# A transformer block on one core: output projection, second norm and feed-forward placed earlier in a software pipeline

## The chip, the cores and the metric

The kernel runs on one core of one Trainium2 chip. The metric is device time in microseconds; the time of the kernel before is the median of three runs. The profile is of one further execution, recorded by the hardware profiler. Engines are called PE (TensorE), DVE (VectorE), ACT (ScalarE), POOL (GpSimd) and SP (SyncE, which here only issues transfers).

## The reference

The input `x` has 16 sequences of 256 rows and 256 columns, all in fp32. One block with the norm ahead of each part is computed:

```
x = x + attention(layernorm(x))      # 16 heads of 16, wq, wk, wv, wo are 256 x 256
x = x + ffn(layernorm(x))            # silu(h @ gate.T) * (h @ up.T) @ down.T, inner size 1024
```

In attention a row `i` sees the columns up to `i + 16`: scores above that are set to minus infinity before the softmax. The weights `gate`, `up` and `down` are not given; each is interpolated (cubic, Catmull-Rom) from a vector of some 2033 control points.

## The kernel before, in words

One sequence is one batch `b`, and its 256 rows are two chunks of 128 partitions. Work on a batch is cut into stages that are functions in the code, and a software pipeline runs different stages of different batches in one step `s` of the main loop (L578). In step `s`, `pb = s` is projected to queries, keys and values; `nb = s - 1` has its row maxima found; `tb = s - 2` has its scores computed transposed, exponentiated and multiplied with the values; `ob = s - 3` is divided by its row sums, projected with `wo`, added to `x` and normed again; the feed-forward follows. The order within a step is written out by hand (L578 to L620), and a helper (`InOrder`, L78) keeps each engine in the order of the program, so no scheduler changes it. That helper issues every instruction, which is why all rows of the profile name L88.

The stages that matter here:

- `inner(nb, tb, g)` for four groups of heads and `outer(nb, tb, g2)` for two pairs: PE computes scores for both batches into two PSUM tiles (`scores`), ACT takes the exponentials (`e`), POOL masks them, DVE finds the maxima (`mx`, the rows `z<-scores`). The next scores overwrite the same PSUM tiles.
- `values` (L383): PE multiplies exponentials with values into `po`, ACT copies it to `au`. `gather` (L402) moves `au` into `den` and `ac` with 12 transfers; `invert` (L418) takes the reciprocal of the row sums and spreads it over partitions through DRAM (`rd`, `rb`); `divide` (L432) multiplies, on DVE: `ac<-ac,rb`.
- `project_o` (L436): PE `py<-wo,ac`, then DVE adds it to `x`. `stats_f` and `norm_f` (L450, L453) compute moments on DVE, a power on POOL (`rstdf`) and the normed `xnf` on DVE. `turn_f` (L456) transposes on PE (`ptf`) and copies to `x2T` on ACT.
- `gate_up(b, i)` (L461), four parts of a batch: PE `pg` and `pu`, ACT tanh (`th`), DVE two products, the last into `inter`. `down(b, c)` (L483), two parts: PE `pd`, DVE adds it to `x`; after the second the output is sent from SP.
- `project_v` (L257): PE `pv`, two ACT copies into `v`. `turn_max` (L372): PE transposes the maxima (`pm`), ACT copies `mxT`, and SP sends it with four transfers into a row of the queries (`qk`) that the scores of the next step read.
- `fill(s, gap)` (L553): what goes into seven numbered gaps between these stages. In the first steps the table `heads` (L541) says how many parts of the weights' interpolation (`pw`) and how many idle matmuls go there; the idle matmuls (`keep_running`, L548, named `run`) multiply the identity and are not used. In later steps `fill` puts parts of `gate_up` there.

Before the change the feed-forward of a batch runs over two steps. Step `s` holds `turn_f(s - 4)` and `gate_up(s - 5, 3)` near its start, `gate_up(s - 4, 0)`, `(s - 4, 1)` and `(s - 4, 2)` further on, and `down(s - 5, 0)` and `down(s - 5, 1)`; the second `down` ends the step. [...]

Of the kernel before, what the change touches and what calls it, by code (L numbers as in the profile page):

```python
# [11 lines left out]
F32 = mybir.dt.float32  # L12
# [6 lines left out]
P = 128  # L19
B, S, DIM = 16, 256, 256  # L20
# [73 lines left out]
def block_kernel(  # L94
# [13 lines left out]
    pe, dve, act, pool, sp = (  # L108
        InOrder(tc, e) for e in (nc.tensor, nc.vector, nc.scalar, nc.gpsimd, nc.sync)
    )  # L110

    const = ctx.enter_context(tc.tile_pool(name="const", bufs=1))
    sb = ctx.enter_context(tc.tile_pool(name="sb", bufs=2))
    sb1 = ctx.enter_context(tc.tile_pool(name="sb1", bufs=1))
    sb3 = ctx.enter_context(tc.tile_pool(name="sb3", bufs=3))
    sb4 = ctx.enter_context(tc.tile_pool(name="sb4", bufs=4))
    sb6 = ctx.enter_context(tc.tile_pool(name="sb6", bufs=6))
    sbx = ctx.enter_context(tc.tile_pool(name="sbx", bufs=10))
    dr = ctx.enter_context(tc.tile_pool(name="dr", bufs=2, space=bass.MemoryType.DRAM))
    ps_s = ctx.enter_context(tc.tile_pool(name="ps_s", bufs=1, space=PSUM))  # L120
    ps_f = ctx.enter_context(tc.tile_pool(name="ps_f", bufs=2, space=PSUM))
# [3 lines left out]
    xs = {}  # L125
# [59 lines left out]
    xns, xnTs, mxs, aus, aos, recs, x2s, x2Ts = ({} for _ in range(8))  # L185
# [25 lines left out]
    def transposed(src, dst, nm):  # L211

        pt = ps_m.tile([P, 2, S], F32, tag="m", name=f"p{nm}")
        for kc in range(2):
            for c in range(2):
                pe.transpose(
                    pt[:, kc, c * P : (c + 1) * P],
                    src[:, c, kc * P : (kc + 1) * P],
                    ident,
                )  # L220
        act.copy(dst, pt)
# [62 lines left out]
    def scores(qk, maxima, g, first, to, n):  # L284

        half = slice(first % P, first % P + HB)
        for r in range(4):
            q4 = slice(32 * r, 32 * r + HD + (0 if maxima else 1))
            on = 0 if maxima else 1
            pe.matmul(  # L290
                tiles[r // 2][half, r % 2, to : to + n],
                lhsT=qk[q4, on, g, first : first + HB],
                rhs=qk[q4, 1 - on, g, 0:n] if maxima else qk[q4, 0, g, S - n : S],
                start=True,
                stop=True,
            )

    def find_max(b, g, r, c, at, n):
        h = 4 * g + r
        seen = sb.tile([P, S], BF16, tag="seen", name=f"z{b}_{h}_{c}")  # L300
        dve.tensor_tensor_reduce(
            out=seen[:, 0:n],
            in0=tiles[r // 2][:, r % 2, at : at + n],
            in1=masks[c],
            scale=1.0,
            scalar=NEG,
            op0=ALU.add,
            op1=ALU.max,
            accum_out=mxs[b][:, c, h : h + 1],
        )  # L310

    def inner(nb, tb, g):
        has_n, has_t = 0 <= nb < B, 0 <= tb < B
        qn, qt = qks[nb % NQK], qks[tb % NQK]
        if has_n:
            if g == 0:
                mxs[nb] = sb.tile([P, 2, H], F32, tag="mx", name=f"mx{nb}")
            scores(qn, True, g, P, S, P + HB + LOOK)
        if has_t:
            scores(qt, False, g, HB, HB - LOOK, S - HB + LOOK)  # L320
        if has_n:
            scores(qn, True, g, P + HB, S, S)
        if has_t:
            scores(qt, False, g, 0, 0, S)
        if has_t:
            for pr in range(2):
                e = sb6.tile([P, 2, S], F32, tag="e0", name=f"e0{tb}_{g}_{pr}")
                act.activation(e, tiles[pr][:, :, 0:S], AF.Exp)

                pool.affine_select(  # L330
                    out=e[:, :, 0:M0], in_=e[:, :, 0:M0],
                    compare_op=ALU.is_ge, fill=0.0, base=LOOK,
                    pattern=[[0, 2], [1, M0]], channel_multiplier=-1,
                )
                es[tb, 0, g, pr] = e
        if has_n:
            for r in range(4):
                find_max(nb, g, r, 1, S, S)
# [115 lines left out]
        x2s[b] = normed(b, "f")  # L454

    def turn_f(b):  # L456
        x2Ts[b] = sb3.tile([P, 2, S], F32, tag="x2T", name=f"x2T{b}")
        transposed(x2s.pop(b), x2Ts[b], f"tf{b}")


# [22 lines left out]
    def down(b, c):  # L483
        inter = inters[b]
        pd = ps_f.tile([P, DIM], F32, tag="f", name=f"pd{b}_{c}")
        for ic in range(8):
            pe.matmul(
                pd,
                lhsT=inter[:, ic, c * P : (c + 1) * P],
                rhs=downT[:, ic, :],  # L490
                start=(ic == 0),
                stop=(ic == 7),
            )
        dve.tensor_tensor(xs[b][:, c, :], xs[b][:, c, :], pd, ALU.add)
        if c == 1:
            sp.dma_start(out[b].rearrange("(c p) d -> p c d", p=P), xs.pop(b))

# [9 lines left out]
    def spline(w, part):  # L507
        at = slice(NPART * part, NPART * part + NPART)
        places = tab_in[:, NPART + P * part : NPART + P * part + P]

        pw = [
            pool_.tile([P, NPART], F32, tag=tag, name=f"pw{w}_{part}_{kc}_{piece}")
            for kc, (pool_, tag) in enumerate(((ps_f, "f"), (ps_m, "m")))
            for piece in range(2)
        ]
        for q in range(4):
            rows = slice(32 * q, 32 * q + 32)
            pe.matmul(
                pw[q], lhsT=places[rows], rhs=cp_in[rows, w, :], start=True, stop=True
            )  # L520
        for kc in range(2):
            first, other, where = pw[2 * kc], pw[2 * kc + 1], second_in[:, kc, at]
            if w < 2:
                to = (gateT, upT)[w][:, kc, at]
            else:

                to = downT[:, kc::2, NPART // 4 * part : NPART // 4 * (part + 1)]
                first, other, where = (
                    t.rearrange("p (o q) -> p q o", q=4) for t in (first, other, where)
                )  # L530
            act.copy(to, first)
            dve.copy_predicated(to, where, other)

    def do(stage, b, *args):
        if 0 <= b < B:
            stage(b, *args)
# [2 lines left out]


    heads = {  # L541
# [3 lines left out]
    }  # L545
    parts = iter([(w, part) for part in range(2) for w in range(2)] + [(2, 0), (2, 1)])

    def keep_running(n):  # L548
        run = ps_f.tile([P, 2 * S], F32, tag="f", name="run")
        for _ in range(n):  # L550
            pe.matmul(run[:, 0:P], lhsT=ident, rhs=ident, start=True, stop=True)

    def fill(s, gap):  # L553

        n, idle = heads.get((s, gap), (0, 0))
        if idle:
            keep_running(idle)
        for _ in range(n):
            spline(*next(parts))
        if gap == 1:  # L560
            do(gate_up, s - 5, 3)
        first = 2 if s >= B else 3
        second = 3 if s >= B else 5 if s == 4 else 4
        if gap == first:
            do(gate_up, s - 4, 0)
        if gap == second:
            do(gate_up, s - 4, 1)


    for t in tiles:  # L570
# [4 lines left out]
    stats_a(0)  # L575
    norm_a(0)
    turn_a(0)
    for s in range(B + 6):  # L578
        pb, nb, tb, ob, db = s, s - 1, s - 2, s - 3, s - 5
        if 3 <= s + 2 < B:  # L580
            load_x(s + 2, sp)
        inner(nb, tb, 0)
        do(values, ob, 1)
        do(gather, ob)
        if s == 1:
            coefficients(2)
        do(turn_f, ob - 1)
        do(stats_a, pb + 1)
        if s == 0:
            for i in range(1, NQK):  # L590
                scores_and_values(i)
        fill(s, 1)
        do(norm_a, pb + 1)
        if s == 0:
            coefficients(0)
            coefficients(1)
        inner(nb, tb, 1)
        do(invert, ob)
        do(project_qk, pb)
        fill(s, 2)  # L600
        outer(nb, tb, 0)
        fill(s, 3)
        inner(nb, tb, 2)
        do(values, tb, 0)
        do(turn_a, pb + 1)
        fill(s, 4)
        do(divide, ob)
        inner(nb, tb, 3)
        fill(s, 5)
        do(down, db, 0)  # L610
        outer(nb, tb, 1)
        do(project_o, ob)
        do(gate_up, s - 4, 2)
        do(stats_f, ob)
        do(norm_f, ob)
        fill(s, 6)
        do(turn_max, nb)
        fill(s, 7)
        do(project_v, pb)
        do(down, db, 1)  # L620


# [27 lines left out]
```

## Time and profile before

| what | value |
|---|---|
| median of 3 runs | 687.26 us (687.01 to 689.21) |
| profiled execution | 685.68 us, its span 684.0 us |
| mean granted PE clock | 0.995 of full |
| idle matmuls (`run`) | 220 records, 30.1 us busy |
| ACT, DVE, POOL busy | 225.5, 357.0, 118.4 us |
| longest single waits of PE by releaser | POOL `ident` 1.4, ACT `upT` 1.0, ACT `downT` 1.0 us |

The span is the time from the first to the last instruction; the execution's own time has 1.7 us more around it. A matmul on fp32 data is recorded as two records, so 16 records of `pd` are 8 matmuls. Records of PE overlap, because the next group starts before the last one's end is reported: the distance between starts tells what a group costs. Busy time of the other engines is an average over the whole span; what matters is which of their results PE waits for and when.

### The profile page before, as it was taken

Reading aid. Unit: us, or ns where it says so; the run is one execution under the profiler, and the core shown is the slowest. Engines: PE = TensorE matmul, PEld = TensorE weight load, DVE = VectorE, ACT = ScalarE, POOL = GpSimd, SP = SyncE. Lnnn points to the kernel's source line nnn. Section 1 sums busy time; section 2 is a strip of 40 time slices with the busy share of each in tenths; the row PEclk is TensorE's granted clock in tenths of the full one; section 3 lists DMA queues with packets and bytes.
Section 4 is the critical chain, followed back from the end, with each engine's and each line's share of the span. In section 5 each row is a group of like instructions: output and inputs, shape, how many; then the busy total and the mean of one; then the engine's idle time right before and its main releaser. Section 6 shows DMA issues by size and latency. Waiting matters only on the chain.

```text
span 684.0 us, 18960 instructions
## 1 busy us (share of the span) xinstructions
PE 670.5 (98%) x7596; PEld 528.3 (77%) x7596; DVE 357.0 (52%) x1473; ACT 225.5 (33%) x413; POOL 118.4 (17%) x244
## 2 busy tenths in 40 slices
PE   7989999999999999999999999999999999999997
PEld 6657777778787777878777787878777787878886
DVE  5656456655654555555555555565554546424431
ACT  2234435342424334242433324242333333241010
POOL 5002222211212111121211111121211112120000
PEclk9899999999999999999999999999999999999999
DMA  6312123130302212130222213021121201011000
GB/s 207 57 24 34 32 54 71 29 63 2 84 13 51 48 43 55 34 63 4 65 33 50 48 38 61 17 66 18 44 39 31 52 20 34 20 32 29 20 16 31
DMA packets 34407, 29.67 MB, mean 43 GB/s; under 512 B 7824, under 2 KB 33680, under 8 KB 34320
## 3 DMA queue, kind: packets, MB, share of 16 engines
q1 hardware_dynamic: 33232, 27.42, 18.3%
q8 instruction: 60, 0.98, 0.6%
q10 hardware_dynamic: 1088, 1.05, 0.5%
q14 instruction: 27, 0.22, 0.1%
HBM read 10.88 MB, written 4.46 MB: 22 GB/s over the span
## 4 chain that ended last, share of the span: by engine, by line
PE 94%; DMA 2%; DVE 1%; POOL 1%; ACT 1%; issue 1%; SPq 0%; DVEq 0%
PE pg L88 16%; PE pd L88 16%; PE pu L88 16%; PE scores L88 15%; PE po L88 7%; PE py L88 5%; PE pq L88 4%; PE pv L88 4%; PE pk L88 4%; PE run L88 3%; PE ptf L88 1%; PE pta L88 1%; PE pw L88 1%; PE pm L88 1%; DMA x<-x 1%
## 5 line engine op out<-in xcount | busy, mean ns | idle before, releaser
L88 DVE CUSTOM_DVE_ANT_0 z<-scores,mask 128x144 bf16<-128x144 f32 (+1 forms) x512 | 154.6, 362 | 124.2 <-ACT e L88 114.4
L88 ACT ACTIVATE e<-scores 128x512 f32<-128x512 f32 (+1 forms) x192 | 107.6, 612 | 208.3 <-PE scores L88 161.5
L88 POOL TENSOR_SCALAR_AFFINE_SELECT e<-e 128x224 f32<-128x224 f32 (+1 forms) x192 | 88.6, 470 | 386.8 <-ACT e L88 380.4
L88 PE MATMUL pg<-x2T,gateT 128*128 128x256 f32 x512 | 122.9, 383 | 0.0
L88 PE MATMUL pu<-x2T,upT 128*128 128x256 f32 x512 | 120.9, 379 | 0.0
L88 PE MATMUL pd<-downT,inter 128*128 128x256 f32 x512 | 116.9, 382 | 0.0
L88 PE MATMUL scores<-qk 17*64 17x144 f32 (+7 forms) x4096 | 112.2, 318 | 2.6 <-DMA qk<-qkc 1.0
L88 PEld LDWEIGHTS pd<-downT,inter 128*128 128x128 f32 x512 | 95.9, 190 | 17.7 <-DVE inter L88 4.2
L88 PEld LDWEIGHTS pu<-x2T,upT 128*128 128x128 f32 x512 | 97.3, 190 | 13.2
L88 PEld LDWEIGHTS pg<-x2T,gateT 128*128 128x128 f32 x512 | 93.7, 190 | 13.9 <-issue 1.0
L88 PEld LDWEIGHTS scores<-qk 17*64 17x64 f32 (+1 forms) x4096 | 71.5, 131 | 40.6 <-issue 31.8
L88 DVE SCALAR_TENSOR_TENSOR th<-th,pg 128x512 f32<-128x512 f32 x64 | 44.0, 688 | 82.5 <-ACT th L88 82.5
L88 ACT ACTIVATE th<-pg 128x512 f32<-128x512 f32 x64 | 38.2, 597 | 110.4 <-PE pg L88 110.4
L88 DVE TENSOR_TENSOR inter<-th,pu 128x512 f32<-128x512 f32 x64 | 44.1, 688 | 25.9 <-PE pu L88 25.8
L88 PE MATMUL po<-e,v 128*32 128x256 f32 (+1 forms) x1024 | 50.0, 336 | 0.0
L88 PEld LDWEIGHTS po<-e,v 128*32 128x32 f32 x1024 | 29.5, 109 | 23.3 <-issue 12.3
L88 DVE DVE_READ_ACCUMULATOR2_ANT mx<- 128x1 f32 x512 | 42.5, 83 | 0.0
L88 DVE TENSOR_TENSOR x<-x,pd 128x256 f32<-128x256 f32 x32 | 13.5, 421 | 53.4 <-PE pd L88 53.4
L88 PE MATMUL pq<-xnT,wq 128*128 128x256 f32 x128 | 33.7, 408 | 0.7 <-ACT xnT L88 0.7
L88 PE MATMUL py<-wo,ac 128*128 128x256 f32 x128 | 31.5, 389 | 1.3 <-DVE ac L88 0.5
L88 PEld LDWEIGHTS pq<-xnT,wq 128*128 128x128 f32 x128 | 24.1, 198 | 9.9 <-issue 5.4
L88 PE MATMUL run<-ident 128*128 128x128 f32 x220 | 30.1, 293 | 1.4 <-POOL ident masks.py:199 1.4
(54 smaller groups left out, 437.0 us busy)
## 6 DMA issues: line engine op xcount, KB each, us to landing
qk<-qkc SPq DMA_DIRECT2D x128, 64.0 KB
x<-x SPq DMA_DIRECT2D x16, 256.0 KB
ac<-au SPq DMA_DIRECT2D x128, 32.0 KB
rb<-rd SPq DMA_DIRECT2D x32, 128.0 KB
out<-x SPq DMA_DIRECT2D x16, 256.0 KB
qk<-mxT SPq DMA_DIRECT2D x64, 4.0 KB
den<-au SPq DMA_DIRECT2D x64, 4.0 KB
cp_in<-cps SPq DMA_DIRECT2D x3, 256.0 KB
```

The costliest lines, as they stand in the source:

```text
L88: return self.tc.keep_in_program_order(fn(*args, **kwargs))
```

## The change

`project_o` and `stats_f` move from behind `outer(nb, tb, 1)` to right behind `inner(nb, tb, 3)`, ahead of gap 5; `norm_f` follows gap 5, ahead of `outer`. `turn_f` no longer runs for the batch of the step before, early in the step, but for the same batch late in the step. `project_v` moves ahead of `turn_max`. The parts of the feed-forward move half a step up: gaps 1, 3 and 4 hold `gate_up` 1, 2 and 3 of batch `s - 4`, gaps 5 and 6 its two `down` parts, and gap 7 `gate_up` 0 of batch `s - 3`, which has just been turned. The loop runs 20 steps instead of 22. In the first steps the interpolation and the idle matmuls are spread differently, with 154 idle matmuls in all instead of 110. `x2T` has two buffers instead of three, `x` nine instead of ten, and the last batch's output is sent in two halves.

```diff
-    sbx = ctx.enter_context(tc.tile_pool(name="sbx", bufs=10))
+    sbx = ctx.enter_context(tc.tile_pool(name="sbx", bufs=9))
...
-        x2Ts[b] = sb3.tile([P, 2, S], F32, tag="x2T", name=f"x2T{b}")
+        x2Ts[b] = sb.tile([P, 2, S], F32, tag="x2T", name=f"x2T{b}")
...
-        if c == 1:
-            sp.dma_start(out[b].rearrange("(c p) d -> p c d", p=P), xs.pop(b))
+        to = out[b].rearrange("(c p) d -> p c d", p=P)
+        if b == B - 1:
+            sp.dma_start(to[:, c, :], xs[b][:, c, :])
+        elif c == 1:
+            sp.dma_start(to, xs.pop(b))
...
     heads = {
-        (1, 1): (1, 4), (1, 3): (1, 8), (1, 4): (0, 8), (1, 5): (1, 4), (1, 6): (1, 6), (1, 7): (1, 8),
-        (2, 1): (1, 0), (2, 3): (0, 10), (2, 5): (0, 8), (2, 6): (0, 8), (2, 7): (0, 8),
-        (3, 3): (0, 10), (3, 5): (0, 8), (3, 6): (0, 4), (3, 7): (0, 4),
+        (0, 7): (0, 18),
+        (1, 1): (1, 2), (1, 3): (1, 8), (1, 4): (0, 8), (1, 5): (1, 4), (1, 6): (1, 8), (1, 7): (0, 14),
+        (2, 1): (1, 0), (2, 3): (1, 8), (2, 5): (0, 10), (2, 6): (0, 20), (2, 7): (0, 14),
+        (3, 3): (0, 16), (3, 5): (0, 4), (3, 6): (0, 8),
     }
...
-        if gap == 1:
-            do(gate_up, s - 5, 3)
-        first = 2 if s >= B else 3
-        second = 3 if s >= B else 5 if s == 4 else 4
-        if gap == first:
-            do(gate_up, s - 4, 0)
-        if gap == second:
-            do(gate_up, s - 4, 1)
+        late = s >= B
+        for what, at in (
+            ((gate_up, s - 4, 1), 1),
+            ((gate_up, s - 4, 2), 2 if late else 3),
+            ((gate_up, s - 4, 3), 3 if late else 4),
+            ((down, s - 4, 0), 4 if late else 5),
+            ((down, s - 4, 1), 5 if late else 6),
+            ((gate_up, s - 3, 0), 7),
+        ):
+            if at == gap:
+                do(*what)
...
-    for s in range(B + 6):
-        pb, nb, tb, ob, db = s, s - 1, s - 2, s - 3, s - 5
+    for s in range(B + 4):
+        pb, nb, tb, ob = s, s - 1, s - 2, s - 3
...
-        do(turn_f, ob - 1)
...
         do(divide, ob)
         inner(nb, tb, 3)
+        do(project_o, ob)
+        do(stats_f, ob)
         fill(s, 5)
-        do(down, db, 0)
+        do(norm_f, ob)
         outer(nb, tb, 1)
-        do(project_o, ob)
-        do(gate_up, s - 4, 2)
-        do(stats_f, ob)
-        do(norm_f, ob)
         fill(s, 6)
+        do(project_v, pb)
+        do(turn_f, ob)
         do(turn_max, nb)
         fill(s, 7)
-        do(project_v, pb)
-        do(down, db, 1)
```

More of the change, by code (lines that the diff above doesn't have):

```diff
@@ L114, in block_kernel @@
     sb1 = ctx.enter_context(tc.tile_pool(name="sb1", bufs=1))
-    sb3 = ctx.enter_context(tc.tile_pool(name="sb3", bufs=3))
     sb4 = ctx.enter_context(tc.tile_pool(name="sb4", bufs=4))
     sb6 = ctx.enter_context(tc.tile_pool(name="sb6", bufs=6))
-    sbx = ctx.enter_context(tc.tile_pool(name="sbx", bufs=10))
+    sbx = ctx.enter_context(tc.tile_pool(name="sbx", bufs=9))
     dr = ctx.enter_context(tc.tile_pool(name="dr", bufs=2, space=bass.MemoryType.DRAM))
```

## The prediction

> **What bounds the kernel now.** I read the page's busy table and clock row first, then three stretches of busy time cut at step borders, then the waits of PE, then the timeline of one step.
>
> ```profile
> PE 670.5 (98%) x7596; PEld 528.3 (77%) x7596; DVE 357.0 (52%) x1473; ACT 225.5 (33%) x413; POOL 118.4 (17%) x244
> PE 94%; DMA 2%; DVE 1%; POOL 1%; ACT 1%; issue 1%; SPq 0%; DVEq 0%
> 0.00:101.03 101.03, 92.74 (x1135) 68.84 (x1135) 55.33 (x253) 33.54 (x62) 22.90 (x50) 0.97 0.30 69
> 101.03:558.62 457.59, 456.82 (x5445) 361.59 (x5444) 253.25 (x1082) 162.77 (x300) 82.10 (x167) 1.00 0.20 42
> 558.62:684.00 125.38, 120.95 (x1019) 97.92 (x1018) 48.45 (x139) 29.16 (x51) 13.41 (x27) 1.00 0.10 27
> 20.00:28.00 8.00, 8.00 (x40) 4.59 (x32) 4.91 (x18) 1.67 (x3) 0.69 (x1) 0.61 0.08 24
> ```
>
> The reader is to see: TensorE is the chain (94%). In the middle stretch (steps 4 to 15) it idles 0.77 us of 457.59, so no order of the same matmuls can win anything there. Idle time lies in the head (101.03 - 92.74 = 8.29 us, plus a stretch at clock 0.61 in 20 to 28 us, worth 8 x 0.39 = 3.1 us) and in the tail (4.43 us, 3.6 of it the last addition and output transfer after the last matmul at 680.4). A full step is 38.93 us (`pv` at 203.50, 242.52, 281.44 in the chain of waits).
>
> The step that matters, from the timeline; columns are start, duration, engine, operation, count, and in brackets the idle time before it and its releaser:
>
> ```profile
> 343.79 0.66 PE L88 MATMUL pta<-ident,xna 128*128 128x128 f32 x4
> 344.28 1.89 PE L88 MATMUL pg<-x2T,gateT 128*128 128x256 f32 x8
> 344.48 0.59 ACT L88 COPY xnT<-pta 128x512 f32<-128x512 f32 x1
> ...
> 347.83 1.04 PE L88 MATMUL scores<-qk 16*64 16x208 f32 x32
> 347.94 0.69 DVE L88 TENSOR_TENSOR inter<-th,pu 128x512 f32<-128x512 f32 x1 [0.41 <-PE pu L88]
> 348.54 0.68 DVE L88 TENSOR_TENSOR ac<-ac,rb 128x512 f32<-128x512 f32 x1
> 348.80 3.72 PE L88 MATMUL pd<-downT,inter 128*128 128x256 f32 x16
> ...
> 353.65 1.97 PE L88 MATMUL py<-wo,ac 128*128 128x256 f32 x8
> ...
> 359.12 1.89 PE L88 MATMUL pv<-wv,xnT 128*128 128x256 f32 x8
> 360.85 1.89 PE L88 MATMUL pd<-downT,inter 128*128 128x256 f32 x8
> 361.05 0.65 ACT L88 COPY v<-pv 128x256 f32<-128x256 f32 x2 [1.37 <-PE pv L88]
> ...
> 638.97 0.69 DVE L88 TENSOR_TENSOR ac<-ac,rb 128x512 f32<-128x512 f32 x1 [2.46 <-DMA rb<-rd]
> 639.71 1.99 PE L88 MATMUL py<-wo,ac 128*128 128x256 f32 x8 [0.48 <-DVE ac L88]
> ```
>
> The division `ac` runs behind the product `inter`, which itself waits for the end of `pu`; it is done at 349.22, while `py` reads it 4.4 us later. At 639 us the two meet: `py` starts 0.05 us after the division ends. A copy out of PSUM starts 0.20 us after the next matmul group has begun (`pta`, `pv`).
>
> **What the Trainium skill says.** "TensorE: Matmul & The Clock Gate", the table at its head: TensorE pulls weight loads ahead of running matmuls, while VectorE and ScalarE are strict first in, first out. The trace agrees: groups of 8 records follow each other every 1.73 us although one is reported at 1.89, and DVE and ACT keep program order. So a late DVE or ACT result holds the matmul that needs it and every matmul behind it. The same page, "Part 1: The HAM clock gate": an idle window of about 3.4 us halves the clock. The trace agrees roughly: after sparse scores at 15.9 to 18.2 us, `pq` takes 3.78 us instead of 1.99.
>
> **The change part by part.** In the built order of instructions the matmuls are the same, apart from idle `run` ones. I price by PE start-to-start times.
>
> *Idle matmuls.* The counts go from 110 to 154 (12 at the start, then the table `heads`): +44, two records each of 112 ns (1.79 us for 16): +9.9 us. What they replace: 18 of them behind step 0 (4.0 us, from 15.0 to 19.0) cover the wait of 0.87 us and the sparse scores (15.9 to 18.2 becomes 0.7 us) and should keep the clock up (-3.1). The 0.79 us wait of `pm` (step 2) and one of the 1.02 us waits behind a spline (step 1) go too. Walking the head: step 1 starts at 19.0 (was 15.9), step 2 at 46.2 (49.0), step 3 at 77.0 (75.4), step 4 at 107.8 with the 0.77 below (101.0). The last has already done 0.5 + 3.45 us of feed-forward (`ptf`, `pg`, `pu`) that before had not: +2.8, or **+2.0 us** without the 0.77. If the clock falls all the same, +5; if more waits vanish, 0.
>
> *Output projection moved right behind `inner(3)`.* Now `py` stands where `pd` stood at 348.80. DVE order is unchanged up to there: last `inter` product, then division. So `py` waits for 349.22 + 0.05: **0.47 us** per full step, and the 0.13 us that it lost before (1.20 instead of 1.07 us from scores to `py`) is absorbed. Behind the waiting `py` is the whole PE queue. Bounds: 0.35 (with the 0.13 returned) to 0.7. The `rb` transfer is no issue in full steps: its last packet lands at 342.9, 14.9 us after the end of `po`, and the division is wanted 19.4 us after it.
>
> *Second norm.* Statistics, the power on POOL (0.69) and the subtraction (0.74) fit beneath `down` and the scores (3.65 + 1.2 + 3.65 us); `xnf` is ready some 5 us early. The addition of `pd`, queued ahead of the subtraction, costs nothing in full steps. Maxima are done about 2.7 us after the outer scores; `down` lies there (3.65). Nothing.
>
> *Value projection, `ptf`, `pm`, then `gate_up` of the same batch.* Let `pv` start at V. It is followed at V+1.73 by `ptf`, at V+2.22 by `pm`, at V+2.44 by `pg`, which needs the copy `x2T`. On ACT two `v` copies stand ahead: V+1.93 to 2.58; then `x2T` 0.59 to V+3.17; `pg` at V+3.21. New wait **0.77 us**; before, `pg` behind `ptf` was another batch's, and its own came 20 us later. `pm` waits about 0.4 of it for the PSUM buffer of `pv`; the same time, not more. Bounds 0.5 (ACT overlap) to 1.0.
>
> *Queues.* `out` (0.38 us of issue) now stands ahead of the four `mxT` transfers on SP, but is released before them. The first of those lands 1.7 us after its copy ends at V+3.53; the scores that read it come after `gate_up` (V+3.2 to 6.7). Covered by 1.4 us. Load of `x` and the smaller pools: a buffer of `x` is still reused three steps after its output was issued, `x2T` and `inter` a step after the last reader. Nothing.
>
> *Steps 4 to 15*: 12 x (0.47 + 0.77 - 0.13) = **+13.3 us**. Step 3: +0.77.
>
> *Steps 16 and 17.* There `down` 0 stands before `py`, and DVE has its addition (0.42) ahead of the division: `down` end +1.3 us against 0.97 and 0.62 us of scores: 0.3 + 0.7. Then `x2T` stands behind two `e` activations (1.19 us) on ACT: `pg` waits 1.3 and 1.45, `ptf` 0.35 once. **+4.1**, less 0.4 that went before.
>
> *Step 18 and the end.* `py` waits for addition and division, 1.3 instead of 0.48 (+0.8; the transfer lands 14.2 us after `po`, nearly the same time). `ptf` waits for `down` 1's addition and the subtraction: 1.0. `pg` waits for `x2T`: 0.83. **+2.6**. Splitting the last output into two transfers of half the size: -0.5 (bounds 0 and -1). Two steps fewer save no PE work.
>
> Sum: 2.0 + 0.8 + 13.3 + 3.7 + 2.6 - 0.5 = +21.9. Walking the whole of PE instead (step 16 at 587.8, 17 at 622.4, 18 at 655.3, 19 at 683.0, last matmul 700.2, then 3.6 to the end as before) gives a span of 703.8, +19.8; I take the walk: it goes by the start-to-start time of each group in its new place, with the 0.1 to 0.2 us that a switch between scores and full matmuls costs, where the sum moves bare groups. The profiled execution took 685.68 us (span 684.0 and 1.7 around it); the median shown is 687.26, 1.6 above. On the median: **707 us**.
>
> **The rivals.**
> A. As above, both new waits in each full step: 707, own range 702 to 712. Chance 0.74.
> B. Only one of the two waits is there. Without the first: 12 x 0.47 less, 701. Without the second: 13 x 0.77 less, 697. For: each hangs on a few tenths in one queue. Against: the order on DVE and ACT is fixed. 0.11.
> C. Both waits, and the scores of the next step also wait for `mxT`, whose packets queue behind the 256 KB of `out`: 0.5 us more in 12 steps, 713. Against: the slack of 1.4 us. 0.07.
> D. Neither wait exists in full steps: 12 x 1.24 less, 692; slower all the same, by head and tail. 0.04.
> E. Faster: no new wait anywhere, since `ac` and `x2T` are there when PE asks, and the head breaks even: 9.9 us of runs against 5.5 us of idle time that can be filled (8.29 less 2.8 of start-up), 3.1 of clock and 1.6 of sparse scores. What is left is the lost 0.13 us in 12 steps, 0.3 of head and 0.5 of output: 685. For: that time is there in the head. Against: it decides only from new waits below 0.2 us a step (12 x 0.2 = 2.4), and I read 1.24. 0.04.
>
> **How the numbers follow.** A measurement here tells 0.3% (2 us) from no change. Faster takes E: 0.04. Same: 0.02, between D and E. Slower: 0.94. The range takes A and B and reaches toward C: 697 to 712; bounds of the waits alone make it 12 x (-0.4 to +0.45), about 5 us each way.
>
> **What would show it.** In the changed profile: `py` waiting for DVE `ac` about 0.5 us a step with PE's start 0.05 us after the division; `pg` waiting for ACT `x2T` about 0.8 us (or shared with `pm` waiting for `v`) a step; a step of some 40 us instead of 38.93; clock near 1.00 in 20 to 28 us; step 4 starting near 107.8. I am wrong if steps stay at 38.8 to 38.9, or if another wait (scores on `mxT`) is the largest.

## The result, and the profile after

| | before | changed |
|---|---|---|
| median of 4 runs | 687.13 us (684.19 to 689.21) | 710.32 us (708.48 to 712.22) |
| ratio | | 1.0341, 95% interval 1.0294 to 1.0388 |
| profiled execution, its span | 685.68, 684.0 us | 712.22, 710.5 us |
| a full step | 38.92 us | 40.20 us |
| last matmul ends | 680.4 us | 707.3 us |

The change makes the kernel 3.4% slower. The kernel before spreads over 5 to 8 us from run to run, and the granted clock goes with it (last section). Each experiment below is compared with runs of the kernel before on the same chip, whose medians lie between 685.07 and 686.80 us; the changed kernel was not run again beside them, so differences to it are told to some 2 us on medians, and better on the steps of the profiles. The profile of the changed kernel is that of its slowest run (712.22).

The page of the changed kernel, part 1 (busy time and share of the span) and the shares of the chain that ended last:

```profile
PE 683.5 (96%) x7684; PEld 537.6 (76%) x7684; DVE 358.3 (50%) x1473; ACT 224.0 (32%) x413; POOL 117.9 (17%) x244
...
PE 92%; ACT 3%; issue 1%; DVE 1%; DMA 1%; POOL 0%; DVEq 0%; ACTq 0%
```

PE has 88 records more, the 44 idle matmuls, and 13.0 us more busy time, but the span grew by 26.5: PE now idles 27.0 us instead of 13.5. In the chain ACT went from 1% to 3%. The waits of PE in the changed kernel (what waited, for whom, us in total, times, longest):

```profile
PE py L88 <- issue: 5.0, 11, 0.5
PE pm L88 <- ACT v L88: 3.9, 13, 0.3
PE py L88 <- DVE ac L88: 3.3, 5, 1.2
PE pm L88 <- DVE mx L88: 2.2, 1, 2.2
PE pg L88 <- ACT x2T L88: 1.4, 2, 0.8
```

Eleven waits of `py` before which the profile shows no releaser ("issue") need the timeline. The same full step of the changed kernel (start, duration, engine, operation, idle time before it; rows of weight loads are left out here and below):

```profile
343.74 1.89 PE L88 MATMUL pv<-wv,xnT 128*128 128x256 f32 x8
...
345.47 0.60 PE L88 MATMUL ptf<-ident,xnf 128*128 128x128 f32 x4
345.67 0.65 ACT L88 COPY v<-pv 128x256 f32<-128x256 f32 x2 [4.15 <-PE pv L88]
346.20 0.60 ACT L88 COPY x2T<-ptf 128x512 f32<-128x512 f32 x1
346.37 0.39 PE L88 MATMUL pm<-ident,mx 128*16 128x128 f32 x2 [0.30 <-ACT v L88]
...
346.86 1.99 PE L88 MATMUL pg<-x2T,gateT 128*128 128x256 f32 x8
...
372.47 1.04 PE L88 MATMUL scores<-qk 16*64 16x208 f32 x32
372.58 0.69 DVE L88 TENSOR_TENSOR inter<-th,pu 128x512 f32<-128x512 f32 x1 [0.41 <-PE pu L88]
373.18 0.68 DVE L88 TENSOR_TENSOR ac<-ac,rb 128x512 f32<-128x512 f32 x1
...
373.97 1.97 PE L88 MATMUL py<-wo,ac 128*128 128x256 f32 x8 [0.46 <-issue]
```

The division ends at 373.86, and `py` starts 0.11 us later: the wait is for `ac`, whatever the label says. Above it, `pg` starts at 346.86, 0.06 us after the end of the copy `x2T` (346.80), which had stood behind the two `v` copies on ACT. Between the starts of `pv` and `pg` lie 3.12 us; by the sum of the groups alone they would be 2.44. Part of this wait stands in the list as `pm` for `v`: in the kernel `pv`, `ptf` and `pm` take turns in two PSUM buffers, so `pm` writes where `pv` was, and it starts 0.05 us after the second `v` copy has ended (346.32).

### The profile page after: what moved, and what is told of

Read it like the earlier page. It is cut to its first block, busy times and chain, and to the rows that moved or that the text cites. A ratio compares the mean times of both kernels' runs of the same rounds, so it can differ in the third digit from the quotient of the medians.

```text
span 710.5 us, 19110 instructions
## 1 busy us (share of the span) xinstructions
PE 683.5 (96%) x7684; PEld 537.6 (76%) x7684; DVE 358.3 (50%) x1473; ACT 224.0 (32%) x413; POOL 117.9 (17%) x244
## 4 chain that ended last, share of the span: by engine, by line
PE 92%; ACT 3%; issue 1%; DVE 1%; DMA 1%; POOL 0%; DVEq 0%; ACTq 0%
PE pg L88 17%; PE pd L88 16%; PE pu L88 16%; PE scores L88 13%; PE po L88 7%; PE run L88 5%; PE py L88 5%; PE pq L88 4%; PE pv L88 4%; PE pk L88 4%; PE pta L88 1%; ACT v L88 1%; ACT x2T L88 1%; PE pw L88 1%; DMA x<-x 1%
## 5 line engine op out<-in xcount | busy, mean ns | idle before, releaser
L88 PE MATMUL pg<-x2T,gateT 128*128 128x256 f32 x512 | 126.8, 391 | 2.8 <-ACT x2T L88 1.4
L88 PE MATMUL scores<-qk 17*64 17x144 f32 (+7 forms) x4096 | 106.9, 317 | 1.0 <-ACT e L88 0.5
L88 PEld LDWEIGHTS scores<-qk 17*64 17x64 f32 (+1 forms) x4096 | 69.2, 131 | 35.9 <-issue 30.4
L88 PE MATMUL run<-ident 128*128 128x128 f32 x308 | 40.5, 290 | 1.4 <-POOL ident masks.py:199 1.4
L88 PEld LDWEIGHTS run<-ident 128*128 128x128 f32 x308 | 38.5, 204 | 3.6 <-POOL ident masks.py:199 1.4
L88 PE MATMUL py<-wo,ac 128*128 128x256 f32 x128 | 33.1, 404 | 8.3 <-issue 5.0
L88 DVE TENSOR_TENSOR x<-x,pd 128x256 f32<-128x256 f32 x32 | 13.5, 421 | 49.2 <-PE pd L88 49.2
L88 PEld LDWEIGHTS py<-wo,ac 128*128 128x128 f32 x128 | 23.9, 196 | 18.0 <-issue 9.7
```

Of the source, the lines that this page charges most:

```text
L88: return self.tc.keep_in_program_order(fn(*args, **kwargs))
```

## Experiments

Short names: *theory* is the two new waits in each full step. A step below is the distance between the `pq` groups of two steps, from step 4 on. It is the same to 0.01 us in all full steps of the changed kernel and of the versions made from it; in the kernel before it is 38.92, with two steps 0.06 and 0.09 longer (the forecast read 38.93).

### 1. Half of down ahead of the output projection

```diff
+        if s < B:
+            fill(s, 5)
         do(project_o, ob)
         do(stats_f, ob)
-        fill(s, 5)
+        if s >= B:
+            fill(s, 5)
         do(norm_f, ob)
```

> The changed kernel with gap 5 (the first half of down) put ahead of project_o in steps 0 to 15; the rest as changed. Theory (two new waits in each full step): py no longer waits for the division, which is done while down runs; 12 x 0.53 = 6.4 us less in steps 4 to 15, and 1 to 2.5 us less in step 3, where four idle matmuls now stand ahead of py and keep the clock up: span some 702 to 703 us instead of 710.5; the wait of pg for x2T stays at about 0.7 us a step. Rival (the loss is head and tail alone, and a wait taken away comes back elsewhere): step stays at 40.2 us, time within 2 us of the changed kernel.

Measured: 703.81 us, ratio to the kernel before 1.0273 (1.0237 to 1.0308), span 702.1; step 39.71, 0.49 less than 40.20. The eleven waits of `py` under "issue" are gone, those of `pm` for `v` are not. Timeline of this kernel:

```profile
367.19 0.69 DVE L88 TENSOR_TENSOR inter<-th,pu 128x512 f32<-128x512 f32 x1 [0.41 <-PE pu L88]
367.80 0.68 DVE L88 TENSOR_TENSOR ac<-ac,rb 128x512 f32<-128x512 f32 x1
368.05 3.72 PE L88 MATMUL pd<-downT,inter 128*128 128x256 f32 x16
...
371.61 1.89 PE L88 MATMUL py<-wo,ac 128*128 128x256 f32 x8
```

DVE runs as before, but now 3.6 us of `down` cover the division. The theory's 6.4 + 1 to 2.5 us were expected, and 8.4 us of span came: 5.9 in the twelve full steps and 2.4 in step 3. There `py` no longer waits and the clock does not fall, but `pm` waits 1.0 us for the maxima instead.

### 2. The norm's transposes ahead of the value projection

```diff
+        do(turn_f, ob)
         do(project_v, pb)
-        do(turn_f, ob)
         do(turn_max, nb)
```

> The changed kernel with turn_f ahead of project_v instead of behind it; nothing else. Theory: the copy x2T then runs beneath pv and ahead of the two v copies, and pm and pg no longer wait: 13 x 0.7 = 9.1 us less (steps 3 to 15), step about 39.45 us, span about 701 us; py still waits for the division. Rival (scores of the next step are late because mxT is): the same time comes back as a wait of the scores for the transfer qk<-mxT, and the step stays at 40.2 us.

Measured: 699.15 us, ratio 1.0211 (1.0172 to 1.025), span 696.1; step 39.37, 0.83 less. Timeline:

```profile
336.83 0.60 PE L88 MATMUL ptf<-ident,xnf 128*128 128x128 f32 x4
...
337.26 1.89 PE L88 MATMUL pv<-wv,xnT 128*128 128x256 f32 x8
337.46 0.59 ACT L88 COPY x2T<-ptf 128x512 f32<-128x512 f32 x1 [2.86 <-PE ptf L88]
...
338.99 0.38 PE L88 MATMUL pm<-ident,mx 128*16 128x128 f32 x2
339.19 0.65 ACT L88 COPY v<-pv 128x256 f32<-128x256 f32 x2 [1.14 <-PE pv L88]
339.21 1.89 PE L88 MATMUL pg<-x2T,gateT 128*128 128x256 f32 x8
```

`x2T` is done at 338.05, beneath `pv`; `pg` follows `pm` at once. From the start of the first of `ptf` and `pv` to `pg` it is 2.38 us instead of 3.12, and the `pg` group, which no longer stands behind a wait, takes 1.73 us to the next instead of 1.83: these two make the 0.83. The scores did not come to wait for `mxT`. Of the 14.4 us of span, 11 are the 13 steps; most of the rest is the clock, which in this profile never fell (1.00), in the changed kernel's twice for 3.4 us.

### 3. Both edits

> Both edits of the two kernels before. Theory: the two waits add, so the gains add: step at 38.8 to 38.9 us as in the kernel before the change, span 693 to 695 us; what is left over the kernel before (8 to 10 us) is head and tail. Rival (the waits shadow each other): the gain is that of the larger alone, about 701 us.

Measured: 693.95 us, ratio 1.0135 (1.0096 to 1.0173), span 692.4; step 38.87. The two waits add: 0.49 + 0.83 = 1.32, and 40.20 - 38.87 = 1.33. Steps 4 to 15 have nothing left, as the busy time between 110 and 590 us shows (stretch, its length, busy PE, PEld, DVE, ACT, POOL, clock, DMA share, GB/s):

```profile
110.00:590.00 480.00, 480.00 (x5676) 380.75 (x5678) 270.42 (x1120) 166.20 (x308) 84.21 (x171) 1.00 0.19 42
```

So the two waits explain the full steps to 0.05 us a step, and 8.4 us over the kernel before remain for head and tail. The smaller pools of `x` and `x2T` are still there in this version, so they cost the full steps nothing that shows.

### 4. The projection's new place alone, in the kernel before

```diff
         inner(nb, tb, 3)
+        do(project_o, ob)
         fill(s, 5)
         do(down, db, 0)
         outer(nb, tb, 1)
-        do(project_o, ob)
```

> The kernel before with one part of the change alone: project_o stands right behind inner(3), ahead of gap 5 and down. Theory (the division sits behind the last product of gate_up on DVE): py waits some 0.5 us in steps 5 to 15, where gap 4 holds a part of gate_up; step 39.3 to 39.4 us instead of 38.92, and some 5 us more in all. No wait in steps 16 and 17, where nothing of gate_up is ahead of the division. Rival (moving the projection costs nothing by itself, only with the rest of the change): step stays at 38.9 us.

Measured: 695.14 us, ratio 1.0128 (1.009 to 1.0166); step 39.32, 0.40 more, as expected. In all it is about 9 us, not 5. The timeline has the rest:

```profile
89.94 0.82 DVE L88 TENSOR_TENSOR ac<-ac,rb 128x512 f32<-128x512 f32 x1 [2.09 <-DMA qk<-qkc]
...
90.85 3.06 PE L88 MATMUL py<-wo,ac 128*128 128x256 f32 x8 [1.83 <-ACT e L88]
...
645.54 1.99 PE L88 MATMUL py<-wo,ac 128*128 128x256 f32 x8 [3.01 <-DVE ac L88]
```

Step 3 has no feed-forward yet, and in step 18, which has no scores left, it was `down` that had covered the transfers from `po` to `rb`. Now `py` waits there (1.8 and 3.0 us, the first under a label that names ACT, though the division ended just ahead of it); after the first the clock fell, and `py` took 3.06 us instead of 1.97. In step 3 `pm` now waits 1.7 us for the maxima as well, since the projection no longer lies between. The expectation had looked at full steps and at 16 and 17 only. In these profiles the full steps cost 4.5 us, step 3 about 4.9 and step 18 about 2.5; 2.8 come back because the clock did not fall near 20 us in this run.

### 5 and 6. The 18 idle matmuls behind step 0, taken away and put into the kernel before

```diff
     heads = {
-        (0, 7): (0, 18),
```

> The changed kernel without the 18 idle matmuls behind step 0 (4.0 us of PE). Theory (they buy the clock): the granted clock falls to half near 19 us for two windows as before the change, step 1 starts about 3 us earlier, and the outer scores of step 1 stand at 27 to 28 us instead of 26.5; in all 0 to 2 us slower than the changed kernel. Rival (they are plain cost): the outer scores of step 1 stand at 23 to 24 us, and the time falls by 3 to 4 us.

> The kernel before with the 18 idle matmuls behind step 0 added, nothing else. Theory (they buy the clock): clock 1.00 in 20 to 28 us, outer scores of step 1 at 26.5 to 27 us instead of 28.0, in all 1 to 1.5 us faster. Rival (plain cost): 3 to 4 us slower.

In the kernel before they stand behind `project_v` of step 0. Without them the changed kernel has 709.74 us (708.83 to 715.14), which can't be told from its 710.32: 4 us of PE work taken away are given back. Its profile is that of the slowest run, 715.14. There the outer scores of step 1 stand at 30.9 us and not at the 27 to 28 expected, because the clock fell twice: from 19.5 to 29.7 us, near the place that the theory names, and from 9.2 to 12.6, ahead of the place of the 18, which can't be their doing. The rival's 23 to 24 us are excluded for this run. With them the kernel before has 684.29 us beside 686.39, ratio 0.9982 (0.9964 to 1.0), outer scores at 26.78; the rival's 3 to 4 us more are excluded. The same 8 us of the two kernels with the 18, which the kernel before spent at clock 0.61 (the column ahead of the DMA share); first the changed kernel:

```profile
20.00:28.00 8.00, 7.60 (x83) 5.15 (x83) 7.08 (x31) 2.27 (x4) 0.69 (x1) 1.00 0.12 33
```

then the kernel before with the 18 added:

```profile
20.00:28.00 8.00, 7.59 (x84) 5.37 (x84) 6.82 (x29) 2.27 (x4) 0.69 (x1) 1.00 0.10 32
```

They buy the clock, at about the price that the clock saves.

### 7. Twenty idle matmuls fewer in the changed kernel

```diff
-        ... (1, 7): (0, 14),
-        ... (2, 6): (0, 20), (2, 7): (0, 14),
+        ... (1, 7): (0, 11),
+        ... (2, 6): (0, 6), (2, 7): (0, 11),
```

> The changed kernel with 20 idle matmuls fewer: gap 7 of step 1 from 14 to 11, gap 6 of step 2 from 20 to 6, gap 7 of step 2 from 14 to 11. Theory (these stand where PE waits for nothing): 20 x 0.224 = 4.5 us less, step 3 starts at about 72.4 instead of 76.8 us, no new wait. Rival (they fill a wait of pm for the maxima and of the scores for mxT): pm or the scores wait instead, and less than 2 us is won.

Measured: 705.63 us, ratio 1.0278 (1.0236 to 1.032), 4.7 us below the changed kernel; step 3 starts at 72.57 us instead of 76.83 (4.26 less), and no new wait of `pm` or of the scores appears in step 2. These were plain cost. Full steps stay at 40.20.

### 8. Both edits, the twenty idle matmuls fewer, and another order of the last steps

The edits of experiments 1, 2 and 7 are in it (the lines of 7 are left out below). In addition `down` is no longer moved ahead in late steps; in steps 16 and 17 the first half of `down` follows `project_o`, and the second follows `turn_f`.

```diff
-            ((down, s - 4, 0), 4 if late else 5),
-            ((down, s - 4, 1), 5 if late else 6),
+            ((down, s - 4, 0), 5),
+            ((down, s - 4, 1), 6),
...
+        ahead = s < B or s == B + 2
+        if ahead:
+            fill(s, 5)
         do(project_o, ob)
         do(stats_f, ob)
+        if not ahead:
+            fill(s, 5)
         do(norm_f, ob)
         outer(nb, tb, 1)
+        if ahead:
+            fill(s, 6)
         do(turn_f, ob)
+        if not ahead:
+            fill(s, 6)
         do(project_v, pb)
         do(turn_max, nb)
```

> Both edits, and in addition 20 idle matmuls fewer in steps 1 and 2 (4.5 us), and the last three steps ordered so that down lies beneath the second norm and beneath the copy x2T. Theory: head 4.5 us shorter than with both edits, the wait of pm for the maxima in step 16 (2.2 us) and the low clock after it (1.7 us) gone, and two or three small waits: span about 681 to 685 us, beside 684.0 of the kernel before. Rival (the idle matmuls stood in place of waits): the head keeps its length, pm or the scores wait instead, and the span is 686 to 690 us.

Measured: 682.23 us (22 runs), ratio to the kernel before 0.9963 (0.995 to 0.9977), span 680.2. Step 38.87; the wait of `pm` for the maxima is gone, and the span is just below the 681 to 685 expected. The gain over the kernel before is one of the clock: in their runs at clock 0.999 or 1.0 the two take the same, 681.9 to 682.4 us here and 682.3 in the three such runs of the kernel before, but 16 of 22 runs are such here and only 3 of 27 there.

### 9. Twenty-seven idle matmuls fewer again

> The fastest kernel so far (both edits, 20 idle matmuls fewer, last steps reordered) with 27 idle matmuls fewer again (6.0 us of PE), in gaps 3, 4 and 6 of step 1, 3, 5 and 6 of step 2 and 3 of step 3. Theory (what is left of idle matmuls fills waits for maxima, exponentials and the rb transfer): the head gets 1 to 3 us shorter, the rest comes back as waits of the scores, of pm and of py, and the clock may fall to half once. Rival (all idle matmuls are plain cost): 6 us less, span 674 us.

Measured: 679.82 us, ratio 0.9908 (0.988 to 0.9936), span 677.0: 3.2 us less than the kernel of experiment 8, about half of the 6.0 us of PE taken away. Two of the waits of PE in this kernel:

```profile
PE scores L88 <- DVE mx L88: 0.7, 3, 0.3
...
PE pm L88 <- DVE mx L88: 0.2, 1, 0.2
```

Scores and `pm` now wait for maxima in the head, 0.7 us together (the third wait of the scores, 0.2 us late in the run, is in the kernel before too). That is less than the 2.8 us given back; this run also came to its first `pq` 0.4 us later, ahead of all edits, and where the rest went is open. In the profile the clock stayed at 1.00; two of the nine runs have 0.997. This is the fastest version of the study: it keeps the change's shorter pipeline, without its two waits, with 107 idle matmuls instead of 154, and beats the kernel before by about 0.9%. In the runs at clock 0.999 or 1.0 alone it takes 678.7 to 680.1 us, beside 682.9 and 683.2 of the kernel before, some 4 us less; the rest of the 7 us is again that its clock falls less often.

## Why the prediction was right, and where it was off

The median was forecast at 707 and came at 710.3; the range held it, and the mechanism was the one named. On the profiled execution the forecast was +19.8 us of span, a span of 703.8, and it is +26.5, or 710.5. Some 3.4 us of the 6.7 between them are two falls of the clock (in steps 3 and 16), where the forecast counted none. The one run of the changed kernel at clock 1.0 took 708.48 us, span 706.8, which is 3.0 off. By stages:

| stage | walk forecast | measured | off by |
|---|---|---|---|
| step 4 starts | 107.8 | 109.3 | +1.5 |
| steps 4 to 15 | 480.0 | 482.0 | +2.0 |
| step 16 | 34.6 | 37.6 | +3.0 |
| steps 17, 18, 19 to the end of the span | 81.4 | 81.6 | +0.2 |

- *Full steps, the wait of `py`.* Forecast 0.47, removed in experiment 1: 0.49. Right, and shown from both sides: experiment 4 adds the same wait to the kernel before.
- *Full steps, the wait of `pg`.* Forecast 0.77, removed in experiment 2: 0.83. Right. A part, 0.30 of the 0.4 forecast, shows as `pm` waiting for `v`.
- *The 0.13 us that was to be absorbed.* Mis-sized, as far as the steps tell: with both waits gone the step is 38.87, only 0.05 below 38.92, though the order there is not quite that of the changed kernel. With the 0.02 and 0.06 of the two waits this makes the net 1.28 instead of 1.11 us a step, the +2.0 above.
- *The head.* Its sign and size were right, but the walk let `py` of step 3 start when PE got there, and checked the `rb` transfer for full steps only. It waited 0.97 us for `ac`, and the clock fell behind it. The division in turn waited 1.35 us for a transfer, by the profile `qk<-qkc`, which it does not read; that it was `rb` is argued from its inputs and not shown. The group takes 3.48 us instead of 1.97, in the changed kernel's timeline:

```profile
95.10 3.48 PE L88 MATMUL py<-wo,ac 128*128 128x256 f32 x8 [0.97 <-DVE ac L88]
```

  Without this wait and the fall, which cost about 2.7 us, step 4 would have started ahead of the 107.8 of the walk: some other part of step 3 was counted about 1 us too long, so that the head comes as close as +1.5 is in part luck. That the 18 runs keep the clock up near 20 us was right (experiments 5 and 6). That the rest of the added runs stand for waits was half right: 20 of them stood for none (experiment 7).
- *Step 16, the step of the forecast that failed.* The text said of the maxima: "`down` lies there (3.65). Nothing." It holds for full steps. In step 16, the last with maxima, the second half of `down` is ahead of the outer scores, so only `ptf` lies between these and `pm` (rows of PE alone):

```profile
619.48 1.14 PE L88 MATMUL scores<-qk 16*64 16x80 f32 x64
620.55 0.71 PE L88 MATMUL ptf<-ident,xnf 128*128 128x128 f32 x4
623.41 0.38 PE L88 MATMUL pm<-ident,mx 128*16 128x128 f32 x2 [2.15 <-DVE mx L88]
623.63 2.81 PE L88 MATMUL pg<-x2T,gateT 128*128 128x256 f32 x8
```

  `pm` starts 2.8 us after the end of the scores' group, about when the text itself had the maxima, and this wait swallowed the one of `pg` for `x2T` (1.3) that was forecast here; behind it the clock fell once more (`pg` 2.81 instead of 1.99). The fall is 1.7 of the +3.0 of this step; the wait alone is 0.85 longer than the one forecast. Experiment 8, which puts `down` back there, has no such wait; it changes other things too, so its time is no measure of this one.
- *Steps 17 and 18.* Small terms: `py` 0.54 (forecast 0.7) and 1.16 (1.3), `ptf` 0.28 and 0.93 (0.35 and 1.0), `pg` 0.76 and 0.67 (1.45 and 0.83). The 1.45 seems to hold the 0.35 as well: `ptf` and `pg` together wait 1.04 in step 17. Terms that were too small and too large meet in the +0.2 of this row.
- *The output in two halves.* Forecast -0.5 in the sum, nothing in the walk. The span ends 3.2 us after the last matmul instead of 3.6, so 0.4 came.
- *The rivals.* B, one of the two waits alone, fell with experiments 1 and 2, and that one wait shadows the other with experiment 3 (they add to 0.01 us). C, that the scores would wait for `mxT`, does not happen in any profile. E, the case for faster, asked for no new wait and a head that breaks even. With the waits gone, the last steps reordered and 47 idle matmuls fewer the moved order does come out ahead (experiment 9), with about as many idle matmuls as the kernel before (107 and 110). So in the full steps it was the placing that lost, not the shorter pipeline. How much of the 0.9% the shorter pipeline itself is worth is not shown: the idle matmuls of the kernel before were not thinned out in the same way.

## What to carry to other kernels

Where one in-order engine has almost no idle time left (here 0.77 of 457.59 us), moving a stage has next to nothing to win (0.05 us a step in experiment 3), and what it loses can be read off before any run: for each moved instruction, write down when its last input is ready on the other engine's own queue, behind what stands there, and compare it with the work that now lies between. Put the producer of a small copy ahead of an unrelated matmul group instead of behind it, and a division behind nothing that waits for the group just ahead. Then do the same sum again for the first and the last steps: their gaps hold other work, and that is where most of what this forecast missed lies.

## What the runs showed that was not expected

The granted clock falls to half for stretches of 3.4 us, or of two or three times that (6.8 in the kernel before, from 19.4 us; 10.2 in experiment 5), and a kernel that PE bounds shows each. Here are the two falls in the profile of the changed kernel (the clock is the column ahead of the DMA share):

```profile
94.00:100.00 6.00, 5.03 (x54) 4.16 (x53) 3.38 (x13) 1.09 (x2) 0.76 (x2) 0.72 0.43 66
618.00:630.00 12.00, 9.85 (x122) 7.29 (x124) 4.56 (x23) 2.99 (x6) 1.92 (x3) 0.86 0.08 25
```

6 x 0.28 and 12 x 0.14 make 1.7 us lost by each. The same comes out of run times: in 22 runs of experiment 8's kernel, 16 with a mean clock of 0.999 or 1.0 took 681.9 to 682.4 us, and the 6 with 0.997 took 683.8 to 684.2, 1.8 us more for what would be one fall. The kernel before ran from 682.3 (clock 1.0) to 690.7 us (0.990).

What brings a fall stays open. The prediction names an idle window as the cause. In these profiles falls came right behind idle times that are shorter than the window it gives: 1.0 us (`py` in step 3 of the changed kernel), 1.8 (the same in experiment 4) and 2.15 (`pm` in step 16), each after scores. The measurement decides here. But the length alone does not decide: the 2.15 us at `pm` were followed by a fall in four profiles (the changed kernel, experiments 1, 3 and 5) and by none in two (experiments 2 and 7), and the 3.0 us of `py` in step 18 of experiment 4 by none. Nor did the waits of 0.3 to 0.6 us in full steps bring one in any profile. Since a fall costs this much, the 18 idle matmuls, 4.0 us of PE, cost nothing measurable over many runs (experiments 5 and 6); in runs in which the clock would have stayed up they do: on the same chip the kernel before takes 682.4 to 682.6 us in its four best runs, and 683.7 at best with the 18 added.

The profile put eleven waits of `py` under "issue", with no releaser, although the division ends 0.11 us ahead in the step shown; taking the cause away removed them all.
